# Expert attention: gate logits computed in the four column strips of TensorE, then one copy and one transpose

## The chip, the cores and the metric

The kernel runs on one core of one Trainium2 chip. The core has five engines that work at the same time and wait for each other by semaphores: TensorE (PE, matrix products into PSUM), VectorE (DVE), ScalarE (ACT), GpSimd (POOL) and SyncE (SP, which issues most loads and stores). Times are microseconds (us) of device time for one execution of the whole program. In the profile a weight load of TensorE is shown apart, as PEld. A float32 matmul is shown as two records, each with its weight load; a transpose is shown as one.

## The reference

The program is a small vision model: a tokenizer, an attention layer with a ReLU score, a second attention that is called expert attention here, a linear attention and a layer of routed experts. Only the expert attention is touched. Its reference, cut to what matters:

```python
# x: (128 images, 64 tokens, 256 features); E = 4 experts, C = 4 chunks of 64 features
mean, var = x.mean(-1, keepdims=True), ((x - mean) ** 2).mean(-1, keepdims=True)
xn = (x - mean) / sqrt(var + EPS) * norm_w
gate = softmax(xn @ router_w.T + router_b)            # (B, T, 4): the gate logits, then their softmax
xc = xn.reshape(B, T, C, 64)
q, k, v = project(xc, qkv_w)                          # for each expert, chunk and one of 2 heads of 32
attn = softmax(q @ k.T / sqrt(32))
y = attn @ v @ proj_w + proj_b                        # for each expert and chunk
out = (y weighted by gate, summed over the experts)   # (B, T, 256)
return x + out @ out_w.T
```

The input of this part has been normalised once more before, which the kernel folds into its factors.

## The kernel before, in words

All of the stream lies in SBUF in `h2`: 128 partitions are the tokens of two images (a pair), and there are 64 pairs of 256 features. `expert_attention` (from L730) works on one pair after the other, and prepares the pairs in blocks of four (`NB = 4`), 16 blocks in all.

**A block's preparation** (class `Block`) has these steps. `statistics` (L812, L813) takes mean and variance of two pairs at a time on DVE. `factors` (L821 to L829) makes nine small steps of them on POOL. `normal` (L835, L838) normalises one pair on POOL and scales the stream. `transpose` (L843) turns half of the features of the four pairs on PE, and `transposed` (L848) copies that half from PSUM to `xT` on ACT. `logits` (L854) makes the gate logits on PE: for each of the four pairs, two matmuls with 128 x 128 of `xT` as weights and the 4 columns of the router `wrs` as the moving side, so that tokens lie on partitions and pairs and experts along the row. `logits_less_max` (L861 to L863, DVE), `exponents` (ACT), `sums` (DVE) and `gates` (POOL) make the softmax over the four experts of each token. `gates_transpose` (L877, PE) and `gates_transposed` (L880, ACT) keep a turned copy of the gates for the bias.

**A pair's own work** (class `Pair`): `queries_keys` (L902, copies by ACT L906), `values` (L914; the first half is copied from PSUM by ACT, the second by DVE, both L923), `scores` (L934), `less_max` (L946, L947 on DVE), `exponents` (L950, ACT), `sums` (L953, L954, DVE), `weights` (L960, L961, POOL, which brings in the gates), `transposed` (L970 on PE, L973 on ACT), `mixed` (L983, copy L991) and `output` (L997, L998, then L999 on DVE adds to the stream; after every fourth pair SP stores four pairs, L1001).

**What sets the order.** The loop over pairs (L1043 to L1075) is written out by hand under `manual_schedule`: each engine runs its instructions in exactly that order. While pair p has its scores and softmax, the pair before it is transposed, mixed and put out, and the next one gets its queries, keys and values. The steps of a block are slipped in by a table: `at(n, place, step)` puts a step into the loop's turn n at a named place. ACT's place comes first in a turn, DVE's after the first half of the sums, ACT2's after it, DVE2's and POOL's after the weights, and PE's last. `n = 4 b` is the turn of a block's first pair, so `n - 2` is two turns earlier. Steps whose turn would be negative go into `do("first")`, which runs ahead of the loop and is not ordered by hand.

**PSUM.** `scores` has its own pool of two tiles (four banks). Every other product takes a bank from the pool `psq` of four, in turn: L843, L854, L877, L902, L914, L970, L983 and L997 share them, and a product waits until the engine that reads the bank's last content is done.

```python
            at(n - 11, "DVE", x.statistics, 0)     # L1016
            ...
            at(n - 4, "PE", x.transpose, 0)        # L1021
            at(n - 3, "ACT", x.transposed, 0)
            at(n - 3, "PE", x.transpose, 1)
            at(n - 2, "ACT", x.transposed, 1)
            at(n - 2, "PE", x.logits)
            at(n - 1, "DVE", x.logits_less_max)
```

Of the kernel before, what the change touches and what calls it, by code (L numbers as in the profile page):

```python
# [11 lines left out]
F32 = mybir.dt.float32  # L12
# [7 lines left out]
P = 128  # L20
# [709 lines left out]
def expert_attention(c, hd, normw, wr, br, wqkv, wvT, wproj, bproj, wout):  # L730
# [3 lines left out]
    tc, nc, h2 = c.tc, c.nc, c.h2  # L734
    SCALE = float(1.0 / np.sqrt(np.float32(32)))
    NP = B // 2
    NB = 4
    with (
# [7 lines left out]
    ):  # L746
        nw = wp.tile([P, 2], F32, name="nw")
        nc.sync.dma_start(nw, normw)
        wrs = wp.tile([P, 2, 4], F32, name="wrs")
        nc.sync.dma_start(wrs, wr.rearrange("(c p) e -> p c e", p=P))  # L750
        brs = wp.tile([P, 4], F32, name="brs")
        nc.sync.dma_start(brs, br.partition_broadcast(P))
        w = wp.tile([P, 2 * D], F32, name="w")
# [17 lines left out]
        for k in range(2):  # L771
            for e in range(4):
                for h in range(2):
                    r = (e % 2 * 2 + h) * 64
# [4 lines left out]
                        start=True,  # L779
                        stop=True,  # L780
# [18 lines left out]
        class Block:  # L799
# [48 lines left out]
                nc.scalar.activation(self.xT[:, fc], self.pt, AF.Copy, scale=nw[:, fc : fc + 1])  # L848

            def logits(self):  # L850
                self.pg = pg = psq.tile([P, NB, 4], F32, tag="pq", name="pg")
                for n in range(NB):
                    for fc in range(2):
                        nc.tensor.matmul(  # L854
                            pg[:, n, :], self.xT[:, fc, n], wrs[:, fc, :], start=(fc == 0), stop=(fc == 1)
                        )

            def logits_less_max(self):
                self.gate = bp.tile([P, NB, 4], F32, tag="gate", name="gate")
                self.gm = gm = np_.tile([P, NB], F32, tag="gm", name="gm")  # L860
                nc.vector.tensor_add(self.pg, self.pg, bcast(brs, 1, NB))  # L861
                nc.vector.tensor_reduce(gm, self.pg, AX.X, ALU.max)
                nc.vector.tensor_sub(self.gate, self.pg, bcast(gm, 2, 4))  # L863
# [146 lines left out]
        def at(n, place, f, *a):  # L1010
            key = (n, place) if n >= 0 else "first"
            work.setdefault(key, []).append(lambda: f(*a))

        for b, x in enumerate(blocks):
            n = NB * b
            at(n - 11, "DVE", x.statistics, 0)  # L1016
            at(n - 10, "DVE", x.statistics, 2)
            at(n - 9, "POOL", x.factors)
            for k in range(NB):
                at(n - 8 + k, "POOL", x.normal, k)  # L1020
            at(n - 4, "PE", x.transpose, 0)  # L1021
            at(n - 3, "ACT", x.transposed, 0)
            at(n - 3, "PE", x.transpose, 1)
            at(n - 2, "ACT", x.transposed, 1)
            at(n - 2, "PE", x.logits)
            at(n - 1, "DVE", x.logits_less_max)
            at(n - 1, "ACT2", x.exponents)
            at(n - 1, "DVE2", x.sums)
            at(n - 1, "POOL", x.gates)
            at(n, "PE", x.gates_transpose)  # L1030
            at(n + 1, "ACT", x.gates_transposed)
# [897 lines left out]
@with_exitstack  # L1929
def vit_tower(ctx: ExitStack, tc: tile.TileContext, a, out):  # L1930
    const = ctx.enter_context(tc.tile_pool(name="const", bufs=1))
    dram = ctx.enter_context(tc.tile_pool(name="dram", bufs=1, space=DRAM))
    c = Ctx(tc, const)

    hd = dram.tile([B, T, D], F32, name="hd")

    hx = dram.tile([B, T, D], F32, name="hx")
    gfd = dram.tile([B * T, 1], F32, name="gfd")
    with tc.tile_pool(name="stream", bufs=1) as sp:
        c.h2 = sp.tile([P, B // 2, D], F32, name="h2")  # L1940
        tokenizer(c, a["x"], a["w1"], a["bn1"], a["w2"], a["bn2"])
        relu_attention(c, a["wqkv0"], a["wmlp"], a["bmlp"])
        expert_attention(
            c, hd, a["normw"], a["wr"], a["br"], a["wqkvf"], a["wvf"], a["wproj"], a["bproj"], a["wout"]
        )
    c.tables(ctx.enter_context(tc.tile_pool(name="tables", bufs=1)))
    with tc.tile_pool(name="gate", bufs=1) as gp:
        k = Routing(c, gp, a["wg"], a["bg"])
        linear_attention(c, hd, hx, out, k, a["wqk1"], a["bqk1"], a["wv1"], a["bv1"], a["wg"])
        experts(c, hx, gfd, out, a["we1"], a["we2"], a["be2"], lambda: route(c, k, gfd))  # L1950
# [68 lines left out]
```

## Time and profile before

| | |
|---|---|
| Runs | 2759.32 us median of 3 (2752.79 to 2761.09) |
| The profiled execution | 2759.04 us; 2757.1 us from its first to its last instruction |
| Expert attention: first scores of pair 0 | 1141.13 us after the span's start |
| Expert attention: scores of the last pair | 1925.29 us |
| PE busy over the whole span | 2599.0 us (94%) |
| DVE, ACT, POOL busy | 2037.6 us (74%), 1627.6 us (59%), 1631.1 us (59%) |

How to read it: the busy shares are means over five stages with different limits. In each row of the timeline stand the start, the length, the engine, the line, the operation with its output and input, and in brackets how long the engine had stood idle before it and what ended that. A wait is listed only where it is longer than 0.15 us. The ends of matmuls are modelled, so that PE can show as busy while it waits; the starts of the weight loads are the better guide.

### The profile page before, as it was taken

The numbers are of one execution on the slowest core, as the hardware profiler recorded it, in microseconds if no ns is written. First come the engines' busy times: TensorE is split into PE (matmuls) and PEld (weight loads), VectorE is DVE, ScalarE is ACT, GpSimd is POOL, SyncE is SP. The second block draws the span as 40 slices with busy tenths as digits, with TensorE's granted clock in tenths as the row PEclk, the third lists the DMA queues.
The fourth block names the chain that finished last, engine by engine and source line by source line (L and its number), as shares of the span: only waits on it lengthen the run. The fifth ranks groups of instructions, "written<-read, shape, count | busy, mean of one in ns | idle before, by whom it ended". The sixth has DMA issues, their size and how long they took to land. (4 is left out here: it accounts for less than half of the span.)

```text
span 2757.1 us, 76948 instructions
## 1 busy us (share of the span) xinstructions
PE 2599.0 (94%) x33263; PEld 1741.0 (63%) x33263; DVE 2037.6 (74%) x3024; ACT 1627.6 (59%) x3415; POOL 1631.1 (59%) x1390
## 2 busy tenths in 40 slices
PE   7989999999999999799999999999699986999997
PEld 3553434434444443688888888888466565888886
DVE  6759999999998989577877777777367685344443
ACT  3228888888898888366666666566245543233332
POOL 3328888898888888656566565553233312454444
PEclk9999999999999999799999999999899995999999
DMA  3000000000000000000000000000424443555554
GB/s 108 32 12 2 2 1 2 2 2 2 1 2 1 2 2 1 12 11 18 11 11 18 11 15 14 10 19 11 115 62 112 102 120 114 180 197 189 188 196 134
DMA packets 138063, 140.80 MB, mean 51 GB/s; under 512 B 107923, under 2 KB 121509, under 8 KB 130032
## 3 DMA queue, kind: packets, MB, share of 16 engines
q1 hardware_dynamic: 126816, 117.91, 14.3%
q0 software_dynamic: 7648, 14.77, 1.7%
q8 instruction: 263, 4.31, 0.7%
q10 hardware_dynamic: 3248, 3.09, 0.4%
q14 instruction: 88, 0.72, 0.1%
HBM read 103.93 MB, written 32.54 MB: 49 GB/s over the span
## 5 line engine op out<-in xcount | busy, mean ns | idle before, releaser
L495 POOL TENSOR_TENSOR m<-q,k 128x1024 f32<-128x1024 f32 x384 | 719.0, 1903 | 30.5 <-PE sc L297 16.1
L487 DVE TENSOR_TENSOR m<-pc,k 128x2048 f32<-128x2048 f32 (+1 forms) x320 | 646.7, 2058 | 0.5 <-ACT q L431 0.5
L297 PE MATMUL sc<-m,wide 128*32 128x512 f32 x4096 | 529.5, 598 | 12.0 <-DVE m L487 7.2
L496 ACT ACTIVATE m<-m 128x1024 f32<-128x1024 f32 x384 | 402.3, 1049 | 6.0 <-POOL m L495 5.4
L297 PEld LDWEIGHTS sc<-m,wide 128*32 128x32 f32 x4096 | 126.4, 109 | 259.7 <-issue 145.6
L505 ACT ACTIVATE m<-k,q 128x64 f32<-128x64 f32 x1024 | 270.8, 339 | 0.8 <-DVE k L378 0.8
L946 DVE TENSOR_REDUCE mx<-sc 128x16 f32<-128x1024 f32 x128 | 156.1, 1220 | 153.9 <-PE sc L934 123.7
L961 POOL TENSOR_TENSOR e<-e,mx 128x1024 f32<-128x1024 f32 x128 | 243.5, 1902 | 10.1 <-POOL mx L960 0.2
L906 ACT COPY qk<-pqk 128x512 f32<-128x512 f32 x256 | 138.9, 604 | 131.7 <-PE pqk L902 131.7
L960 POOL TENSOR_TENSOR mx<-mx,gate 128x16 f32<-128x16 f32 x128 | 27.6, 216 | 314.5 <-ACT z L991 151.2
L1853 PE MATMUL ph<-xt,w1s 128*128 128x256 f32 x896 | 201.1, 383 | 4.2 <-DVE xt L1844 3.4
L1869 PE MATMUL po<-w2s,hT 128*128 128x256 f32 x896 | 198.0, 379 | 0.0
L973 ACT COPY pT<-pt 128x512 f32<-128x512 f32 x256 | 138.7, 599 | 98.9 <-PE pt L970 98.1
L1853 PEld LDWEIGHTS ph<-xt,w1s 128*128 128x128 f32 x896 | 171.7, 192 | 29.5 <-DVE xt L1844 4.2
L1869 PEld LDWEIGHTS po<-w2s,hT 128*128 128x128 f32 x896 | 168.1, 190 | 21.7
L902 PE MATMUL pqk<-xT,w 64*128 64x128 f32 x2048 | 168.9, 288 | 2.1 <-issue 2.0
L947 DVE TENSOR_TENSOR e<-sc,mx 128x1024 f32<-128x1024 f32 x128 | 156.8, 1225 | 4.4
L1887 POOL DMA_INDIRECT out<-y,rout x56 | 56.7, 1013 | 168.6 <-ACT hT L1857 131.3
L1857 ACT ACTIVATE hT<-ph,w1s 128x256 f32<-128x256 f32 x224 | 93.3, 470 | 104.0 <-PE ph L1853 104.0
L902 PEld LDWEIGHTS pqk<-xT,w 64*128 64x128 f32 x2048 | 142.2, 189 | 19.7 <-issue 10.7
L953 DVE TENSOR_REDUCE mx<-e 128x16 f32<-128x1024 f32 x128 | 153.2, 1197 | 1.7 <-ACT e L950 1.7
L970 PE MATMUL pt<-ident,e 128*128 128x128 f32 x1024 | 142.1, 279 | 6.4 <-POOL e L961 2.8
(302 smaller groups left out, 4976.0 us busy)
## 6 DMA issues: line engine op xcount, KB each, us to landing
w1s<-in_we SPq DMA_DIRECT2D x30, 1028.0 KB, 5.3
w2s<-in_we SPq DMA_DIRECT2D x30, 1024.0 KB, 4.9
hd<-h SPq DMA_DIRECT2D x16, 512.0 KB, 3.2
x<-hd SPq DMA_DIRECT2D x16, 512.0 KB, 3.8
h<-hd SPq DMA_DIRECT2D x4, 2048.0 KB, 12.9
hx<-h SPq DMA_DIRECT2D x4, 2048.0 KB, 11.7
out<-h SPq DMA_DIRECT2D x4, 2048.0 KB, 20.5
xt<-in_x SPq DMA_DIRECT2D x15, 512.0 KB, 3.5
```

Of the source, the lines that this page charges most:

```text
L297: nc.tensor.matmul(dst[j : j + 32], wide[:, hf, s : s + 32], part, start=start, stop=stop)
L487: nc.vector.tensor_tensor(m, bcast(self.pq[:, hf, i : i + n], 3, T), k, ALU.max)
L495: nc.gpsimd.tensor_tensor(m, bcast(self.q[:, hf, s : s + 2], 3, T), k, ALU.subtract)
L496: nc.scalar.activation(m, m, AF.Relu)
L505: nc.scalar.activation(self.parts[i, hf][:, q], self.blk.k[:, hf, i], AF.Relu, bias=self.q[:, hf, i - NB // 2, q : q + 1], scale=-1.0,)
L902: nc.tensor.matmul(pq[par][:, k, eh, :], w[r, f : f + P], self.xT[r, fc], start=True, stop=True)
L946: nc.vector.tensor_reduce(mx, sc, AX.X, ALU.max)
L947: nc.vector.tensor_sub(e, sc, bcast(mx, 2, T))
L953: nc.vector.tensor_reduce(self.sm[x], self.e[x], AX.X, ALU.add)
L961: nc.gpsimd.tensor_mul(e, e, bcast(sm, 2, T))
L1853: nc.tensor.matmul(ph[:, j], self.w1[:, w0 : w0 + P], self.xt[:, fc], start=(fc == 0), stop=(fc == 1))
L1869: nc.tensor.matmul(po, self.hT[:, f, r * P : r * P + P], self.w2[:, f, :], start=(f == 0), stop=(f == 7))
```

## The change

The gate logits are computed the other way round. The router's 4 columns, padded with zeros to 32 (`wrs` is now 128 x 2 x 32, cleared by POOL first), are the weights, and 128 tokens of `xT` are the moving side. Each of the block's four pairs has its own strip of 32 columns of the array, and writes the experts to its own 32 partitions of one PSUM tile `pl`. ACT copies `pl` to SBUF (`logits_copied`), and one matmul with `lg` as weights and 16 chosen columns of the identity (`logits_transpose`) gives `pg` in the same form as before, so that everything from `logits_less_max` on is unchanged. To make room for the two new steps, all steps of the preparation up to the logits move one turn earlier.

```diff
-        wrs = wp.tile([P, 2, 4], F32, name="wrs")
-        nc.sync.dma_start(wrs, wr.rearrange("(c p) e -> p c e", p=P))
+        wrs = wp.tile([P, 2, 32], F32, name="wrs")
+        nc.gpsimd.memset(wrs, 0.0)
+        nc.sync.dma_start(wrs[:, :, 0:4], wr.rearrange("(c p) e -> p c e", p=P))
 ...
             def logits(self):
-                self.pg = pg = psq.tile([P, NB, 4], F32, tag="pq", name="pg")
-                for n in range(NB):
-                    for fc in range(2):
+                self.pl = psq.tile([P, P], F32, tag="pq", name="pl")
+                for fc in range(2):
+                    for n in range(NB):
                         nc.tensor.matmul(
-                            pg[:, n, :], self.xT[:, fc, n], wrs[:, fc, :], start=(fc == 0), stop=(fc == 1)
+                            self.pl[n * 32 : n * 32 + 32],
+                            wrs[:, fc, :],
+                            self.xT[:, fc, n],
+                            start=(fc == 0),
+                            stop=(fc == 1),
                         )
+            def logits_copied(self):
+                self.lg = np_.tile([P, P], F32, tag="lg", name="lg")
+                nc.scalar.copy(self.lg, self.pl)
+
+            def logits_transpose(self):
+                self.pg = psq.tile([P, NB, 4], F32, tag="pq", name="pg")
+                some = c.ident.rearrange("p (n r) -> p n r", r=32)[:, :, 0:4]
+                nc.tensor.matmul(self.pg, self.lg, some, start=True, stop=True)
 ...
-            at(n - 11, "DVE", x.statistics, 0)
-            at(n - 10, "DVE", x.statistics, 2)
-            at(n - 9, "POOL", x.factors)
+            at(n - 12, "DVE", x.statistics, 0)
+            at(n - 11, "DVE", x.statistics, 2)
+            at(n - 10, "POOL", x.factors)
             for k in range(NB):
-                at(n - 8 + k, "POOL", x.normal, k)
-            at(n - 4, "PE", x.transpose, 0)
-            at(n - 3, "ACT", x.transposed, 0)
-            at(n - 3, "PE", x.transpose, 1)
-            at(n - 2, "ACT", x.transposed, 1)
-            at(n - 2, "PE", x.logits)
+                at(n - 9 + k, "POOL", x.normal, k)
+            at(n - 5, "PE", x.transpose, 0)
+            at(n - 4, "ACT", x.transposed, 0)
+            at(n - 4, "PE", x.transpose, 1)
+            at(n - 3, "ACT", x.transposed, 1)
+            at(n - 3, "PE", x.logits)
+            at(n - 2, "ACT", x.logits_copied)
+            at(n - 2, "PE", x.logits_transpose)
             at(n - 1, "DVE", x.logits_less_max)
```

## The prediction

> **What bounds the kernel now.** The page first: TensorE (PE) is the busiest engine, and a strip of the array already works in this kernel (L297, 128x32 weights, 512 columns). In section 1 the count of PE is read, in section 5 the busy time: 4096 records in 529.5 us are 0.129 us each although one lasts 0.598, so four run side by side.
>
> ```profile
> PE 2599.0 (94%) x33263; PEld 1741.0 (63%) x33263; DVE 2037.6 (74%) x3024; ACT 1627.6 (59%) x3415; POOL 1631.1 (59%) x1390
> ...
> L297 PE MATMUL sc<-m,wide 128*32 128x512 f32 x4096 | 529.5, 598 | 12.0 <-DVE m L487 7.2
> ```
>
> Then the table by stretches, at the start of the expert stage and in its middle (PE, PEld, DVE, ACT, POOL, then the granted clock near the end): PE is full in the middle, and cold at the start (0.57).
>
> ```profile
> 1100.00:1140.00 40.00, 26.85 (x412) 21.06 (x412) 10.71 (x38) 7.10 (x13) 24.45 (x38) 0.57 0.08 19
> ...
> 1380.00:1480.00 100.00, 99.38 (x2359) 84.59 (x2361) 77.83 (x114) 62.30 (x113) 60.97 (x70) 1.00 0.05 14
> ```
>
> The groups of that stage, for the line that changes:
>
> ```profile
> L854 PEld LDWEIGHTS pg<-wrs,xT 128*128 128x128 f32 x224 | 27.2, 192 | 0.7
> L854 PE MATMUL pg<-wrs,xT 128*128 128x4 f32 x224 | 25.8, 247 | 0.0
> ```
>
> A busy PE hides waits, so the timeline decides. I number the pairs of a block of four 0 to 3 and measure each from its first score load (L934) to the next.
>
> ```profile
> 1414.02 0.57 PEld L843 LDWEIGHTS ptx<-ident,xn 128*128 128x128 f32 x4
> 1414.14 1.22 DVE L923 COPY v<-pv 128x512 f32<-128x512 f32 x2
> ...
> 1414.88 0.95 PEld L970 LDWEIGHTS pt<-ident,e 128*128 128x128 f32 x8 [0.29 <-issue]
> ...
> 1416.00 1.46 PEld L934 LDWEIGHTS sc<-qk 32*64 32x64 f32 x128 [0.17 <-issue]
> ...
> 1426.21 1.97 PEld L854 LDWEIGHTS pg<-wrs,xT 128*128 128x128 f32 x16
> ...
> 1428.02 0.94 PEld L970 LDWEIGHTS pt<-ident,e 128*128 128x128 f32 x8
> ...
> 1429.12 1.46 PEld L934 LDWEIGHTS sc<-qk 32*64 32x64 f32 x128 [0.17 <-issue]
> ...
> 1437.60 0.19 PEld L914 LDWEIGHTS pv<-wvp,xT 64*64 64x64 f32 x2 [0.34 <-DVE gate L863]
> ...
> 1441.49 1.46 PEld L934 LDWEIGHTS sc<-qk 32*64 32x64 f32 x128 [0.17 <-issue]
> ...
> 1450.70 1.22 DVE L923 COPY v<-pv 128x512 f32<-128x512 f32 x2
> ...
> 1453.42 1.46 PEld L934 LDWEIGHTS sc<-qk 32*64 32x64 f32 x128 [0.17 <-issue]
> ```
>
> Pair 2 (ends with the logits) takes 13.12 us, pair 3 12.37, pair 0 11.93, and pair 1, to the next start at 1465.62, 12.20: 49.62 a block, and most blocks repeat it to 0.01. A pair without extras, near the stage's end:
>
> ```profile
> 1902.50 1.46 PEld L934 LDWEIGHTS sc<-qk 32*64 32x64 f32 x128 [0.17 <-issue]
> ...
> 1911.71 1.22 DVE L923 COPY v<-pv 128x512 f32<-128x512 f32 x2
> ...
> 1912.76 0.97 PEld L970 LDWEIGHTS pt<-ident,e 128*128 128x128 f32 x8
> ...
> 1913.89 1.46 PEld L934 LDWEIGHTS sc<-qk 32*64 32x64 f32 x128 [0.17 <-issue]
> ```
>
> It takes 11.39. VectorE (DVE) is a close second: its two value copies start 9.21 after the scores and free the two PSUM banks that the next transposes (L970) need. With the block statistics (L812, L813, 1.10 us) in the pair they start at 10.3, and the transposes wait: 0.74 from copy to load (1414.14 to 1414.88), 1.12 to the scores, so about 12.2. That is pair 1 now: 11.39, 0.44 for L843, 0.36 of waiting. Pair 2 has the statistics too, but its logits cover them. Pair 3's 0.98 over 11.39 are waits on banks, since the logits hold one of four until L863.
>
> **The change, part by part.** *Logits.* 16 records of 128x128 weights go (1426.21 to 1428.02, 1.81 us). In their place stand 16 records with 128x32 weights and 128 columns in four strips. From below: a quarter of L297's 0.129 is 0.032, times 16 is 0.52. From above: no overlap, 16 at 0.113 as now, 1.81, and two switches of 0.2 (last transpose load to first score load is 0.31 at 1428.82 to 1429.12, against 0.11 between transposes), 2.2. I take 0.8, since L297 is the same shape of weights, with switches. The Trainium skill (TensorEngine Tiling (Array Packing), Key Properties) says that a change of tiling mode drains the engine and gives no price, which speaks against the change. The 0.31 is such a place; without any drain the logits would cost 0.52 by the same rows.
>
> *Transpose back.* One matmul, two records: 0.23 at L854's pitch of 0.113, 0.43 at L998's 0.215. It has 16 columns, so I take 0.23.
>
> *Copy.* One ScalarE (ACT) copy, between L880's 0.25 and L991's 0.39, first in ACT's queue of pair 2. Behind it are the copies of pT, which wait for L970, later on PE than the logits. Hidden; without that cover 0.4 x 15 = 6 us.
>
> *Everything earlier by one pair.* This is what costs. The statistics move from pairs 1 and 2 to 0 and 1, L843's second half to pair 0, its first half to pair 3, the logits to pair 1. By the changed program's order and waits, pair 0's L843 needs the bank of the first DVE value copy, and L970 that of the second.
>
> - Pair 0: copies start at 9.21 + 1.10 = 10.31; L843 at 11.05; L970 after the second copy, 10.31 + 1.22 + 0.13 = 11.66; scores at +1.12 = 12.78. I take 12.75, +0.81. If the statistics hid, 11.94.
> - Pair 1: DVE floor 12.2; PE 11.39 + 0.8 = 12.19. I take 12.25, +0.05 (at 2.2 for the logits 13.6, +1.4).
> - Pair 2: no statistics; 11.39 + 0.23 = 11.62, -1.50.
> - Pair 3: the logits' bank is held as before; 12.37 + 0.44 = 12.81, +0.44.
>
> Sum -0.20 a block: twelve full blocks give -2.4. The last two whose pairs prepare a block have no statistics left: pair 0 stays, pair 1 +0.16 (12.03 to 12.19), pairs 2 and 3 as above, -0.9; the very last has no L843 in pair 3 either, -1.4.
>
> What moves along costs nothing where its cover stays. POOL: pair 2's weights end 0.75 into pair 3, then a normal step of 2.46 and the factors of 3.93 (1444.17 to 1448.10) run to 7.1, before the weights at 8.0: 0.9 to spare, beyond that the next transposes would wait. ACT: the xT copies (0.69) stay first in the queue, in pairs 0 and 1 instead of 1 and 2, ahead of the same pT copies. DVE: L861 comes 7.9 into pair 3, long after the transpose back. The moved steps issue no DMA, and SP's one store a block (L1001) is not passed.
>
> *The start.* Before, block 1's L843 came in pairs 0 and 1. Now its first half stands on PE ahead of pair 0's L902, and waits for POOL's fourth normal of block 1.
>
> ```profile
> 1134.96 1.35 PEld L902 LDWEIGHTS pqk<-xT,w 64*128 64x128 f32 x10
> ...
> 1139.09 2.43 POOL L835 TENSOR_SCALAR xn<-h,mv,ra 128x256 f32<-128x256 f32 x2
> ...
> 1141.13 1.46 PEld L934 LDWEIGHTS sc<-qk 32*64 32x64 f32 x128 [0.39 <-issue]
> ```
>
> POOL has it at 1141.52, 0.1 later with the new memset. Then: transposes 0.3; 16 records of L902 at 0.158 (ten took 1134.96 to 1136.54) 2.5; from there to the scores as before 4.6; two waits for a bank that block 1's transposes now hold, about 0.6 each, 1.2. Scores at 1150.2 instead of 1141.13: +9. From below, at the warm rate of 0.061 and without bank waits, +6.3; from above +10.5. The load of wrs on SP now follows the memset, which POOL runs at 1115.6, and SP issues the load at 1116.06: nothing. Pair 0 of the first block took 11.27 and becomes 12.75; with +0.05, -1.50 and +0.44 the first block gives +0.5.
>
> Sum: 2759.04 (profiled, span 2757.1 and 1.9 around; the median of the runs is 2759.32) + 9.0 + 0.5 - 2.4 - 2.3 = 2763.8, so **2764**. The saved PE time is spent waiting on DVE and at the start.
>
> **Rivals.**
> - A. The statistics hide in pair 0 after all: -0.81 on thirteen pairs, -10.5 in sum, 2753. For it: DVE is only 78% busy. Against: pair 1 waits for exactly this now.
> - B. Faster: as A, and the start costs nothing because something else already held pair 0: 2744. From a start cost under 6 us and A together it decides. Against: POOL's end at 1141.5 stands 6.6 after L902's second part.
> - C. The strips take turns: pair 1 at about 13.5, +1.25 on 15 pairs, 2783. Against: L297.
> - D. More bank waits than I count in pairs 0, 1 and 3, some 0.4 to 0.6 a block: 2770 to 2773. For it: the same program has three free banks of four for most of pair 3, and a wait on DVE in each of the other pairs but 2.
>
> **How the numbers follow.** The sum as worked out 0.50, A 0.17, B 0.07, C 0.06, D 0.20. What a measurement of this kernel can tell from no change is about 0.3%, 8.3 us: faster is under 2751, slower over 2767.6. B and a little of A are faster, 0.10; C, most of D and a tenth of the main case slower, 0.31; the rest 0.59. The range takes A's end, D and the bounds of the start: 2752 to 2775.
>
> **What would show it.** First scores near 1150; pairs of 12.75, 12.25, 11.6, 12.8, with PE idle before L843 of pair 0 and DVE value copies ending that wait; new logits under 1 us a block; the transpose 0.2 to 0.25. Wrong if pair 0 is 11.9 (A), the first scores come before 1147 (B), or a group of logits takes 1.8 (C).

## The result, and the profile after

The changed kernel takes 2765.91 us (median of 17 runs, 2757.45 to 2772.41), the kernel before 2758.2 on the same chip (17 runs, 2749.43 to 2762.21). The ratio is 1.0028, with a 95% interval of 1.0017 to 1.0039: 7.7 us more (2758.2 x 0.0028), clear of the noise, and just inside the 8.3 us that the prediction called no change. The forecast was 2764. The profiled execution spans 2764.6 us (2757.1 before), 7.5 us more.

The start first, from the timeline of TensorE's weight loads in the profile after (start, length, engine, line, operation; in brackets the idle time ahead and what ended it). After, the lines have other numbers: L845 transposes xn, L857 is the new logits, L872 the transpose back, L918 the queries and keys, L930 the values, L950 the scores, L986 the transposes of e; L939 on DVE and ACT copies the values.

```profile
1140.44 0.18 PEld L845 LDWEIGHTS ptx<-ident,xn 128*128 128x128 f32 x1 [3.44 <-POOL xn L837]
1141.65 0.18 PEld L845 LDWEIGHTS ptx<-ident,xn 128*128 128x128 f32 x1 [1.02 <-POOL xn L837]
1142.05 1.79 PEld L918 LDWEIGHTS pqk<-xT,w 64*128 64x128 f32 x16 [0.22 <-issue]
...
1150.10 1.46 PEld L950 LDWEIGHTS sc<-qk 32*64 32x64 f32 x128 [0.39 <-issue]
```

PE waits for POOL's normal steps of block 1 (3.44, then 1.02 us) before it may touch the first pair's queries. First scores at 1150.10; before, 1141.13: 8.97 us.

One block in the same timeline:

```profile
1414.22 0.42 PEld L845 LDWEIGHTS ptx<-ident,xn 128*128 128x128 f32 x4 [0.71 <-DVE v L939]
...
1415.89 1.46 PEld L950 LDWEIGHTS sc<-qk 32*64 32x64 f32 x128 [0.17 <-issue]
...
1425.67 0.41 PEld L1014 LDWEIGHTS po<-bn,gT 128*128 128x128 f32 x2
1426.41 0.38 PEld L857 LDWEIGHTS pl<-xT,wrs 128*32 128x32 f32 x16 [0.33 <-issue]
1426.99 0.86 PEld L986 LDWEIGHTS pt<-ident,e 128*128 128x128 f32 x8 [0.20 <-issue]
1428.01 1.46 PEld L950 LDWEIGHTS sc<-qk 32*64 32x64 f32 x128 [0.17 <-issue]
...
1438.22 0.41 PEld L872 LDWEIGHTS pg<-ident,lg 128*128 128x128 f32 x2
...
1439.58 1.43 PEld L950 LDWEIGHTS sc<-qk 32*64 32x64 f32 x125 [0.17 <-issue]
1441.69 0.19 PEld L950 LDWEIGHTS sc<-qk 32*64 32x64 f32 x3 [0.69 <-issue]
...
1451.00 0.58 PEld L845 LDWEIGHTS ptx<-ident,xn 128*128 128x128 f32 x4
...
1452.62 1.46 PEld L950 LDWEIGHTS sc<-qk 32*64 32x64 f32 x128 [0.17 <-issue]
...
1463.62 0.42 PEld L845 LDWEIGHTS ptx<-ident,xn 128*128 128x128 f32 x4 [0.71 <-DVE v L939]
...
1465.30 1.46 PEld L950 LDWEIGHTS sc<-qk 32*64 32x64 f32 x128 [0.17 <-issue]
```

From score load to score load, pair 1 takes 12.12, pair 2 11.57, pair 3 13.04 and pair 0 12.68. Pair 0 shows the wait of its transposes for DVE's value copy (0.71). Pair 3 shows something new: after 125 of its 128 score loads PE stops for 0.69 us, and the profile names no cause ("issue").

The medians over all blocks, from the same starts, are 12.68, 12.16, 11.56 and 12.80, 49.2 a block (49.62 before). The saving is real, but it is not what the whole stage shows. Counted from the traces, after minus before:

| Stretch | us |
|---|---|
| up to the first scores | +8.97 |
| pairs 0 to 3 (50.21 to 49.06) | -1.15 |
| pairs 4 to 47, the usual lengths (11 blocks) | -4.5 |
| pairs 4 to 47, what single pairs take beyond the usual (3.95 to 8.95) | +5.0 |
| the other pairs, and the program after the last scores | -0.7 |
| sum | +7.6 |

The fourth line was in no term of the sum. The table of waits (engine and line waiting, for what; us in all, times, longest) shows it, first before:

```profile
PEld sc L934 <- issue: 11.5, 58, 1.3
PEld pqk L902 <- issue: 9.1, 43, 1.2
```

and after, over the same 710 us:

```profile
PEld sc L950 <- issue: 17.4, 65, 1.6
PEld pqk L918 <- issue: 11.8, 49, 1.2
```

In front of scores and queries PE stands still for 8.6 us more, with nothing to wait for. Most single waits in these rows are the usual 0.17 to 0.22 ahead of a new shape of weights; the extra ones are 0.4 to 1.6 long. Summed over pairs 4 to 47, stalls of over 0.39 us make 3.8 before and 9.0 after; over pairs 1 to 62, 6.7 and 12.9.

### The profile page after: what moved, and what is told of

It reads as the page before. It is cut to its first block, busy times and chain, and to the rows that moved or that the text cites. A ratio compares the mean times of both kernels' runs of the same rounds, so it can differ in the third digit from the quotient of the medians.

```text
span 2764.6 us, 77031 instructions
## 1 busy us (share of the span) xinstructions
PE 2590.3 (94%) x33295; PEld 1722.6 (62%) x33295; DVE 2038.5 (74%) x3024; ACT 1632.5 (59%) x3431; POOL 1631.3 (59%) x1391
## 5 line engine op out<-in xcount | busy, mean ns | idle before, releaser
L918 PE MATMUL pqk<-xT,w 64*128 64x128 f32 x2048 | 169.2, 288 | 5.0 <-issue 4.6
L918 PEld LDWEIGHTS pqk<-xT,w 64*128 64x128 f32 x2048 | 142.2, 188 | 23.2 <-issue 14.6
L986 PE MATMUL pt<-ident,e 128*128 128x128 f32 x1024 | 143.1, 281 | 3.4 <-POOL e L977 1.2
```

The lines of the kernel that those rows point to most:

```text
L918: nc.tensor.matmul(pq[par][:, k, eh, :], w[r, f : f + P], self.xT[r, fc], start=True, stop=True)
```

## The experiments

Runs of one kernel scatter by up to 16 us, and the profiled ones reach this stage at different times (first normal step between 1112 and 1121 us). Traces are therefore compared from POOL's first normal step of the stage on. The table has, for each kernel: from that step to the first scores; the usual block (sum of the four median pairs); the stalls over 0.39 us in pairs 4 to 47; from that step to the last scores; from there to the span's end; and the ratio of the runs to those of the kernel before on the same chip.

| Kernel | first scores | block | stalls | last scores | rest | ratio, interval |
|---|---|---|---|---|---|---|
| before | 20.3 | 49.62 | 3.8 | 804.5 | 831.8 | 1 |
| after | 29.2 | 49.21 | 9.0 | 812.4 | 831.4 | 1.0028 (1.0017 to 1.0039) |
| e1, block 1 late | 17.6 | 49.17 | 5.3 | 803.6 | 832.2 | 1.0011 (0.9995 to 1.0027) |
| e2, no statistics in pair 0 | 30.9 | 48.49 | 10.1 | 806.6 | 834.7 | 1.0006 (0.9991 to 1.0022) |
| e3, the move alone | 32.5 | 50.14 | 5.8 | 824.9 | 831.5 | 1.0096 (1.0074 to 1.0119) |
| e4, strips in place | 18.3 | 48.73 | 9.8 | 797.9 | 835.2 | 1.0005 (0.9990 to 1.0020) |
| e5, the same, spread | 18.3 | 48.38 | 9.2 | 794.9 | 834.1 | 0.9977 (0.9964 to 0.9990) |
| e6, factors later | 17.8 | 48.37 | 8.1 | 791.7 | 835.4 | 0.9966 (0.9952 to 0.9980) |
| before, 128 loads on | 26.0 | 49.61 | 4.2 | 810.9 | 833.5 | 1.0027 (1.0013 to 1.0041) |
| after, 128 loads on | 28.5 | 49.22 | 8.6 | 814.2 | 834.5 | 1.0037 (1.0023 to 1.0051) |
| strips in place, 128 on | 23.8 | 48.73 | 9.0 | 804.3 | 834.6 | 0.9993 (0.9977 to 1.0008) |
| after, 64 loads on | 30.8 | 49.17 | 8.9 | 810.2 | 831.8 | 1.0019 (1.0004 to 1.0034) |
| before, 64 loads on | 22.4 | 49.62 | 5.8 | 807.9 | 834.1 | 1.0010 (0.9998 to 1.0021) |
| e5, 64 loads on | 17.2 | 48.49 | 4.4 | 789.7 | 834.4 | 0.9949 (0.9934 to 0.9965) |

### The move alone, and the strips alone

In the kernel after, with the old logits where they were and the rest a turn earlier:

```diff
-            at(n - 3, "PE", x.logits)
-            at(n - 2, "ACT", x.logits_copied)
-            at(n - 2, "PE", x.logits_transpose)
+            at(n - 2, "PE", x.logits)        # the form of before: xT as weights
```

> The kernel after with the old logits (xT as weights, sixteen loads of 128x128, result in its final layout, no copy and no transpose back), which stand at the end of pair 2 as before; statistics, factors, normal steps and transposes of xn keep the earlier turns. So it is the earlier turns alone, without the strips. Theory M (the move costs the start and pair 0, the strips are what gains): first scores at 1150, pairs 0 to 3 of 12.7, 11.7 to 12.2, 13.1 and 12.8, 50.3 to 50.8 a block against 49.2 in the kernel after; 2780 to 2787. Rival N (the move gains by itself, as the statistics no longer stand in pair 2 and the logits were hidden by bank waits): no more than 49.4 a block, 2762 to 2768.

Measured: pairs of 12.68, 11.53, 13.13 and 12.80, 50.14 a block, ratio 1.0096, 26 us more than before (the trace shows 20.4 of them up to the last scores). N falls. M holds in kind, though its 50.3 to 50.8 was a little too much. Without the strips the earlier turns cost 0.52 us a block (50.14 - 49.62) and the start.

The other half, in the kernel before (a new place "PE0" stands between `old.transposed(0)` and `cur.scores()`):

```diff
             at(n - 2, "PE", x.logits)
+            at(n - 1, "ACT", x.logits_copied)
+            at(n - 1, "PE0", x.logits_transpose)
...
                 if old:
                     old.transposed(0)
+                do((p, "PE0"))
                 cur.scores()
```

> The kernel before with the new logits in strips, their copy and the transpose back, but with every other step in the turn that it had before: logits at the end of pair 2, copy first on ACT in pair 3, transpose back in pair 3 behind the first eight transposes of e and ahead of the scores. So it is the strips alone, without the earlier turns. Theory M (the strips gain about 1 us a block, the earlier turns cost the start): first scores at 1141.1, pairs 0 and 1 as before (11.94, 12.19), pair 2 at 12.2 (11.39 + 0.8, and the floor by DVE's statistics is 12.2 as well), pair 3 at 12.4 to 12.7; about 0.5 to 0.9 a block less than before, 7 to 13 us less, 2745 to 2751. Rival W (without the earlier turns the copy cannot be hidden: PE waits for ACT in pair 3): pair 3 at 13.2 or more, no gain, 2756 to 2762. The stalls of PE for which the profile shows no cause may shift either by up to 6 us.

Measured: pairs of 11.93, 12.19, 12.25 and 12.36 (13.12 and 12.37 for the last two before): 0.89 a block less, and the transpose back costs nothing in pair 3, since that pair waits for a bank anyway. So W falls and M holds for the lengths of the pairs. The time did not follow: ratio 1.0005. The trace gives 6.6 us less up to the last scores (eleven blocks at 0.89 would alone be 9.8), 6 us having gone into the stalls (9.8 instead of 3.8), and 3.4 more come after the last scores; that leaves 3.2 less in this execution, inside the interval of the runs.

### The start

The kernel after, with block 1 alone in its old turns:

```diff
-            at(n - 5, "PE", x.transpose, 0)
+            m = n + 1 if b == 1 else n
+            at(m - 5, "PE", x.transpose, 0)
...
-            at(n - 2, "PE", x.logits_transpose)
+            at(m - 2, "PE0" if b == 1 else "PE", x.logits_transpose)
```

> The kernel after, but the preparation of block 1 alone stays in the turns that it had before: its transposes in pairs 0 and 1 of the first block, its logits in pair 2, the copy and the transpose back at the start of pair 3. Theory S (the 9 us are the price of putting block 1's first transposes, which wait for POOL's fourth normal step, ahead of the first pair's queries): first scores at 1141.1 instead of 1150.1, the later blocks as in the kernel after, about 9 us less than the kernel after, 2757. Rival G (the start is given back later, because the first block then pays for the transposes in its pairs): first scores at 1141.1, but the first block's four pairs together at least 5 us longer, 2762 or more. Rival O (something else at the start, such as the new memset or the load of wrs): first scores stay after 1147, time within 3 us of the kernel after.

Measured: first scores 17.6 after the first normal step (29.2 after, 20.3 before). O falls, and S is right on the start. But part is given back in the very next pair, which took 16.21 instead of 12.05. POOL's timeline of this run:

```profile
1139.31 1.23 POOL L837 TENSOR_SCALAR xn<-h,mv,ra 128x256 f32<-128x256 f32 x1
1140.64 1.23 POOL L840 TENSOR_SCALAR h<-h,rs,mr 128x256 f32<-128x256 f32 x1
1141.84 0.21 POOL L889 TENSOR_TENSOR gate<-gate,gm 128x16 f32<-128x16 f32 x1
```

and PE's:

```profile
1142.10 0.09 PEld L893 LDWEIGHTS pgt<-ident,gate 128*16 128x16 f32 x1 [5.26 <-POOL gate L889]
```

PE waits 5.26 us for the first gates (L889). The earlier turns had put block 2's first normal step (L837, L840) ahead of them on POOL. From the first normal step to the gates it is 29.4 us here (1112.45 to 1141.84) and in the kernel after, 26.8 in the kernel before. In the kernel after nobody sees it, because PE comes even later. To the second pair's scores it is 31.6 us before, 41.3 after, 33.8 here. The move of PE's steps thus cost 7.4 of 9.7, the rest stayed. G's mark, a first block at least 5 us longer, is met too: its four pairs take 54.99 us here and 49.05 in the kernel after. But 11.6 us were gained ahead of them, so the fifth pair's scores come 72.6 us after the first normal step, against 78.3 in the kernel after and 70.5 in the kernel before. S thus has the larger part and G a part. The intervals of the runs (1.0011 against 1.0028) overlap and separate the two no further.

### Pair 0

The kernel after, its statistics one pair at a time:

```diff
-            at(n - 12, "DVE", x.statistics, 0)
-            at(n - 11, "DVE", x.statistics, 2)
+            at(n - 13, "DVE", x.statistics, 0)      # each step now takes one pair
+            at(n - 11, "DVE", x.statistics, 1)
+            at(n - 11, "DVE", x.statistics, 2)
+            at(n - 10, "DVE", x.statistics, 3)
```

> The kernel after, with the block statistics one pair at a time: one in pair 3 of the block before, two in pair 1, one in pair 2, none in pair 0 (two in pair 0 and two in pair 1 in the kernel after). Theory D (pair 0 is long because the statistics delay DVE's value copies, whose banks the transposes of xn wait for): pair 0 falls from 12.68 to about 11.94, pair 1 stays at 12.1, pair 2 at 11.6, pair 3 between 12.8 and 13.3; 0.2 to 0.7 a block less, 3 to 10 us less than the kernel after, 2756 to 2763. Rival E (pair 0 is long because PE has the transposes of xn and of the gates there): pair 0 stays above 12.5, time no less than the kernel after or up to 8 us more, since pairs 2 and 3 take statistics as well.

Measured: 11.93, 12.16, 11.59 and 12.80. Pair 0 lost the 0.74 that were expected, to 0.01, and pairs 2 and 3 took a statistic each for nothing. PE's transposes of xn in pair 0, in this run's timeline:

```profile
1403.29 0.47 PEld L845 LDWEIGHTS ptx<-ident,xn 128*128 128x128 f32 x4
1403.72 0.91 PEld L986 LDWEIGHTS pt<-ident,e 128*128 128x128 f32 x8
1404.80 1.46 PEld L950 LDWEIGHTS sc<-qk 32*64 32x64 f32 x128 [0.17 <-issue]
```

The wait for DVE's value copy is gone from the first line. E falls. In the runs it is 1.0006 against 1.0028, 6 us with an uncertainty of about 5; the stalls made 10.1 us (9.0 in the kernel after).

### The stalls without a cause

Their places have a pattern in every trace. They come 103 to 151 weight loads after a pair's first score load (the scores are 128 loads, the first queries the next 16), and return one block later 8 to 10 loads further on. To test whether the place in PE's instruction stream is what counts, the products at the start of the stage (`pwv`) were written several times into the same tile:

```diff
-        for k in range(2):
+        for k in [0] * 8 + [0, 1]:      # 64 matmuls, 128 loads; [0] * 4 for half of it
             for e in range(4):
```

> The kernel before with 64 more matmuls at the start of the stage, where PE waits anyway: the same products written again into the same tile. Result and schedule are the same, but all later instructions of PE stand 64 weight loads (128 instructions) further on in its stream. Theory F (PE's stalls without a cause in the profile sit at fixed places of the instruction stream, near weight loads number 11777, 12934, 14090 and so on, 1157 apart, and cost according to what PE runs there; the kernel before had 6.7 us of them in the block pairs, the kernel after 13): the stalls stay near these numbers, now at other instructions, and their sum moves by 2 us or more, most likely up; the usual pair periods stay at 11.93, 12.19, 13.12 and 12.37. Rival T (the stalls belong to a tile, a pair or a moment): they stay at the same instructions of the same pairs, and the sum stays within 1 us of 6.7.

> The kernel after with the same 64 matmuls more at the start of the stage. Theory F: stalls near the same load numbers, their sum moves by 2 us or more from 13, most likely down, and the time with it; the usual pair periods stay at 12.68, 12.12, 11.57 and 12.80. Rival T: same instructions, sum within 1 us of 13. The start may be up to 2 us later, since the added matmuls take some 4 us where PE waits.

> The strips in place (earlier kernel's turns) with the same 64 matmuls more. That run's pairs were 0.89 a block shorter than before's, which is some 12 us, but its time was not, and its stalls summed to about 14 us. Theory F: stalls near the same load numbers, their sum moves by 2 us or more, most likely down, and the time follows: 2750 or less. Rival T: sum within 1 us of 14 and the time as that run's.

Measured: 4.2, 8.6 and 9.0 us of stalls instead of 3.8, 9.0 and 9.8, nearly all in the same pairs, and there at the same instructions (a few small ones came or went). F, as it was put, failed in all three and T was met, with sums in pairs 4 to 47 within 1 us. So the stalls are no accident of one execution: they repeat. But the count shows why this did not decide: the distances of the stalls are multiples of about 127.5 loads (in the kernel after 255, 892 and 1147 or 1148 loads, which is 2, 7 and 9 times), and 128 was a whole period. The 1157 and 128.5 loads in the expectations are a little off: a block of 1139 loads and the 8 to 9 by which a stall moves on are nine times 127.5. The times of these runs say little about the stalls; in the kernel before the added matmuls came to 5.7 us in front of the first scores (26.0 instead of 20.3), and that is most of its 1.0027. The "64 weight loads" of the first expectation were wrong, since a float32 matmul has two.

Half a period, with the places worked out beforehand:

> The kernel after with 32 more matmuls at the start of the stage (64 weight loads, 128 instructions of PE). The shift by 128 loads left the stalls at the same instructions, but the stall numbers in these traces are multiples of about 128.5 loads apart (a block of four pairs is 1139 loads, the same stall returns 8 to 9 loads further on in the next block), so that shift was a whole period and decided nothing; this one is half a period. Theory F (stalls sit at every 128.5th load of the stream and cost only where that place falls on the last scores and the first queries of a pair, 103 to 146 loads after the pair's first): the stalls leave pairs 6, 10, 14, 18 (third of the block) and 15, 19, 23 (fourth) and come in pairs 8, 12, 16 (first of the block, from load 124 on) and 13, 17, 21 (second, from load 105 on) and so on, sum anywhere between 5 and 12 us. Rival T (they belong to the code of a pair): same pairs, 116 and so on, sum 8.5 to 9 in pairs 4 to 47. The usual pair periods stay 12.68, 12.12, 11.57, 12.80 in both.

> The kernel before with the same 32 matmuls more. In pairs 4 to 47 it had 3.8 us of stalls, and 4.2 with the whole period's shift, in pairs 6 and 10 and in 33 to 45. Theory F: they come in other pairs and the sum changes; pairs of the four that have to wait for DVE or a bank anyway take up part. If it stays under 5 us, the kernel before has fewer for a reason of its own (its pairs 2 and 3 wait for banks or run the 1.81 us of logits where the stream can be fetched ahead) and not by its place; if it is 7 to 10 us, it was the place. Rival T: same pairs, 3.8 to 4.4.

> The strips in place with the statistics spread, and the same 32 matmuls more. Without them the stalls were 9.2 us in pairs 4 to 47, in pairs 19, 23, 27 (fourth of the block) and 41 most. Theory F: other pairs, sum 5 to 12 us, the time moves by as much against that run's ratio of 0.9977. Rival T: same pairs, same sum, ratio 0.9977 to 0.9985.

Measured in the kernel after: the stalls left pairs 6, 10, 14, 18, 15, 19 and 23 and came in pairs 8, 17, 21, 25, 33, 38, 42, 46 and 47, at loads 128, 116, 125, 133 and so on, as worked out for 8, 17 and 21; in 12, 13 and 16, which were named too, none over 0.39 us came. Pair 15 in the kernel after, with the stall behind its load 108:

```profile
1337.92 1.29 PEld L950 LDWEIGHTS sc<-qk 32*64 32x64 f32 x108 [0.17 <-issue]
1340.02 0.31 PEld L950 LDWEIGHTS sc<-qk 32*64 32x64 f32 x20 [0.81 <-issue]
```

and pairs 15 and 17 in the shifted kernel, the first now whole and the second broken behind load 116:

```profile
1328.99 1.46 PEld L950 LDWEIGHTS sc<-qk 32*64 32x64 f32 x128 [0.17 <-issue]
...
1354.48 1.36 PEld L950 LDWEIGHTS sc<-qk 32*64 32x64 f32 x116 [0.17 <-issue]
1356.76 0.22 PEld L950 LDWEIGHTS sc<-qk 32*64 32x64 f32 x12 [0.93 <-issue]
```

T falls, and F holds for the places in the kernel after. What arrives there can be seen in the DMA view of the kernel after, 1337 to 1339.5 us:

```profile
DMA packets 1, 0.02 MB, mean 7 GB/s; under 512 B 0, under 2 KB 0, under 8 KB 0
## 3 DMA queue, kind: packets, MB, share of 16 engines
q8 instruction: 1, 0.02, 3.1%
```

The only transfer in it is a packet of 16 KB of instructions, 1337.34 to 1338.59; PE goes on at 1340.02. Such a packet landed 1.1 to 1.6 us before PE resumed at each of the 107 stalls of over 0.39 us in pairs 4 to 47 of all fourteen traces.

Whose packets these are follows from their number. From the first scores to the last, 783 us, the kernel after loads 17838 weights on PE, which is 139.9 times 127.5, and 140 packets of 16 KB arrive (the other 23 packets of instructions have 8 KB and another queue). So there is one to each border, as every place 127.5 loads behind the last is called here, and they are PE's own. Matched in order, PE passes the border at each of its 14 stalls in pairs 1 to 62 between 1.1 and 1.6 us after the landing of its packet, and the 125 borders without a wait 4.0 us after it in the median, only 9 of them within 1.6. PE thus stops where it comes to a border too early for its next instructions. A fast stretch just ahead (128 score loads in 1.46 us) brings it there early; that a slower stretch or a wait for a bank hides the rest fits the places, but no run tests it alone. What PE still does in the 1.1 to 1.6 us after the landing is not seen either.

In pairs 4 to 47 the kernel before had 3.8 to 4.2 us of stalls, and 5.8 at half a period, when they fell in pairs 9 to 30 instead of 6, 10 and 37 to 45. That lies between the bounds of its expectation, under 5 for a reason of its own and 7 to 10 for the place, and decides between neither. Over pairs 1 to 62 the three shifts (none, 128 and 64 loads) give 6.7, 7.8 and 7.0 us before and 12.9, 12.5 and 10.0 after: the changed kernel has more at every place that was tried, and why is not shown. For e5 the sum in pairs 4 to 47 went from 9.2 to 4.4 at half a period, below the 5 to 12 that F gave, and here the runs came out shorter too.

### A version that beats both

The strips in the turns of before, and the statistics spread over pairs 1, 2 and 3:

```diff
-            at(n - 11, "DVE", x.statistics, 0)
-            at(n - 10, "DVE", x.statistics, 2)
+            at(n - 11, "DVE", x.statistics, 0)      # each step now takes one pair
+            at(n - 10, "DVE", x.statistics, 1)
+            at(n - 10, "DVE", x.statistics, 2)
+            at(n - 9, "DVE", x.statistics, 3)
```

> The strips alone in the earlier kernel's turns (as in the run of the strips in place), and the block statistics spread: one in pair 1, two in pair 2, one in pair 3, instead of two in pair 1 and two in pair 2; the factors stay in pair 3, after them. Theory D (statistics delay DVE's value copies and so the transposes): pair 1 falls from 12.19 to 11.83 (PE's own work), pair 2 stays at 12.25, pair 3 rises by no more than 0.2 over 12.36; 0.2 to 0.4 a block less than the strips in place, 2 to 5 us less than that run's stage. Rival E (pair 3, held by a bank until the gates, takes the 0.55 of one statistic in full): 12.9 in pair 3 and no gain.

Measured: 11.94, 11.83, 12.25 and 12.36. D holds to 0.01: pair 1 fell to PE's own work, and pair 3 took the statistic for nothing. Ratio 0.9977 (0.9964 to 0.9990), faster than before, 6.3 us. With the half period of added matmuls on top it is 0.9949 (0.9934 to 0.9965), 14 us. Of the 7.7 us between the two, which are uncertain by some 5.5, the trace shows 3.5 in pairs 4 to 47 (538.3 instead of 541.8), though it does 32 matmuls more. This is the lowest ratio of the table; its interval touches that of e5 and overlaps that of the last run.

The last run moved block 2's factors behind the first pair's weights, in e5:

```diff
-            at(n - 9, "POOL", x.factors)
+            at(0 if b == 2 else n - 9, "POOL", x.factors)
```

> The strips in place with the statistics spread, and the factors of block 2 alone in the first pair's turn, behind its weights, instead of ahead of its gates. Reason: in all traces POOL runs the normal steps of block 1, the factors of block 2 and then the first pair's gates in one chain, 26.8 us from the first normal step to the gates (29.4 where the earlier turns put block 2's first normal step there too), and the first pair's end waits for it. Theory P (POOL's chain sets the end of the first pair): the gates come 3.9 us earlier, the second pair's scores 2 to 3.9 us earlier counted from the first normal step, about 0.1% less than that run: ratio 0.996 to 0.9975. Rival Q (PE or ACT ends there as late, or the first pair's factors then delay its successors): less than 1 us.

Measured: the gates come 23.1 after the first normal step instead of 26.8, but the second pair's scores only 29.9 instead of 31.3. The gates came earlier as P said, but the gain, 1.4, lies between P's 2 to 3.9 and Q's less than 1, so neither holds as put. It is no larger than the scatter: the strips in place, with the factors where they were, had the second pair's scores at 30.4. PE's next waits there, in this run:

```profile
1139.94 0.09 PEld L893 LDWEIGHTS pgt<-ident,gate 128*16 128x16 f32 x1 [1.33 <-issue]
1140.37 0.71 PEld L845 LDWEIGHTS ptx<-ident,xn 128*128 128x128 f32 x4 [0.34 <-ACT v L939]
1142.06 1.57 PEld L986 LDWEIGHTS pt<-ident,e 128*128 128x128 f32 x8 [0.98 <-POOL e L977]
```

ACT's value copies are late next: POOL's weights wait 2.46 us for them. Ratio 0.9966 against 0.9977, which the intervals do not separate.

## Why the prediction was right, point by point

The time was right to 2 us, 2764 against 2765.9; the difference was forecast as 4.8 us and came as 7.7 (7.5 in the profiled executions). The start, which is the largest term, and the order of the pairs' lengths were right as worked out. That the sum came so close is in part luck: stalls of PE that stand in no term cost 6.2 us (12.9 against 6.7 in pairs 1 to 62), and the pairs apart from stalls came out some 3 us shorter in all than forecast.

- **New logits**, 0.8 taken: 1426.08 (end of the loads ahead) to 1426.99 (next transposes) is 0.91, against 0.11 between two groups of transposes, so 0.8; pair 1, which holds them, takes 12.12 where a plain pair takes 11.39, so 0.73. The groups of the stretch after show the parts:

```profile
L857 PEld LDWEIGHTS pl<-xT,wrs 128*32 128x32 f32 x224 | 5.3, 109 | 4.6 <-issue 4.6
L872 PEld LDWEIGHTS pg<-ident,lg 128*128 128x128 f32 x28 | 5.3, 190 | 0.7
L867 ACT COPY lg<-pl 128x128 f32<-128x128 f32 x14 | 3.7, 266 | 28.3 <-PE pl L857 28.3
```

  Each of the 14 groups of logits waits 0.33 (4.6 / 14) before its first load, and 0.20 follows ahead of the next transposes (1426.99 in the block above). The sixteen loads between take 0.38 in all, 0.024 a piece though one lasts 0.109, so the strips run side by side and C falls. The Trainium skill (TensorEngine Tiling (Array Packing), Key Properties) says that a change of tiling mode drains the engine; this trace agrees in so far as there is a gap on either side, 0.53 together, which is more than the loads take.
- **Transpose back**, 0.23: pair 2 takes 11.57 where a plain pair takes 11.39, so 0.18. In pair 3 it costs nothing (strips in place).
- **Copy** (266 ns, between the two bounds) hidden: right.
- **Pairs**: 12.75, 12.25, 11.62 and 12.81 were forecast, 12.68, 12.12 to 12.16, 11.56 and 12.80 came, so 0.41 to 0.46 a block less instead of 0.20. Pairs 0 and 1 were each taken some 0.1 too high. The floor of 12.2 that DVE's statistics were to set in pair 1 is not there: with the same statistics and without the logits that pair took 11.53 (the move alone), so the logits alone made its length. The cause of pair 0 is shown by the run without its statistics, so A is out: 11.93 is the length with the statistics elsewhere.
- **Start**: 1150.2 forecast, 1150.10 measured, in the order that was worked out. This is better than the working deserves: among the traces with the earlier turns, first scores came 28.5 to 32.5 after the first normal step. B is out. That POOL also has one more normal step ahead of the first gates was missed; behind PE's own delay it costs nothing.
- **First block**: +0.5 forecast, -1.15 measured. The sum took only the usual 1.50 off pair 2 of the first block; that pair fell from 14.45 to 11.57, since it had one of the stalls (1.15 us) before and has none after. Pair 0 came out at 12.05 instead of 12.75, and pair 1 at 12.64 instead of 12.17.
- **What failed** is the silent assumption of the sum that PE's usual pairs make the stage. In pairs 4 to 47 the kernel after loses 8.95 us beyond its usual lengths, before 3.95, and in the pairs behind them the stalls make 3.9 us after and 1.7 before, which used up most of the 2.3 us that the sum put there. Rival D had the size of the loss (0.4 to 0.6 a block) but not its nature: no more bank waits came than were counted.

## What to carry to other kernels

Work that is moved earlier is paid where the pipeline starts, and by these runs this move (1.0096 alone), not the strips (1.0005 alone), made the kernel slower: there the work that used to come in good time stands at the head of an in-order queue, and behind it the next queue (POOL here) has its own version of the same delay. Where a change takes as little as here (0.4 of 49.6 us a block) from a stage of many small instructions, read the waits without a cause and their distances in instructions before believing a sum of durations; the same code can gain or lose several us by where it stands in the stream (9.2 against 4.4 us of stalls in one kernel here). To test a suspected period, shift by half of it, not by the whole.

## What was not expected of the hardware

PE stood still for 0.4 to 2.2 us where no engine or DMA transfer of data held it, at multiples of about 127.5 weight loads (a load and its matmul each) of its program. One 16 KB packet of instructions arrives for each 127.5 loads (140 in the stage), and in each stall that packet had landed 1.1 to 1.6 us before PE went on. Adding 32 matmuls that do nothing new took such stalls from 9.2 to 4.4 us in one kernel, and in another moved them and left their sum at 8.9 instead of 9.0.
